# A graph network on one core: the attention of the second layer scaled by its sums on ScalarE, block by block, with other opening loads and a new order of steps

## The chip, the core and the metric

The kernel runs on one core of one Trainium2 chip. Its time is the device time of one execution in microseconds (us); the figure to be compared is the median of several executions. The core's engines each work through their own instruction queue, in order: TensorE (PE in the profile, PEld for its weight loads), VectorE (DVE), ScalarE (ACT), GpSimd (POOL) and SyncE (SP), which here issues nearly all DMAs.

## What is computed

`x` is 128 graphs of 128 nodes with 256 features in fp32; `adj` holds zeros and ones. Two layers follow each other. Cut to what matters:

```python
# layer 0, a graph transformer: 8 heads of 32
q, k = x @ Wq + bq, x @ Wk + bk
attn = softmax(q k^T / sqrt(32))
out  = sum over r of (attn * (adj == r)) @ (x @ Wv[r] + bv[r])
x = ln(x + out @ Wo + bo)
x = ln(x + gelu(x @ W1 + b1) @ W2 + b2)          # 256 -> 1024 -> 256
# layer 1: two graph attentions, then a feed-forward part
def gat(h, W, a):
    Wh = h @ W
    e = leaky_relu(Wh @ a[:256] + (Wh @ a[256:])^T, 0.2)
    att = softmax(where(adj > 0, e, -9e15), axis=1)
    return att @ Wh
h = ln(x + gat(gat(x, W1, a1), W2, a2))
out = ln(h + relu(h @ w_ff1 + b_ff1) @ w_ff2 + b_ff2)
```

## The kernel before

**Tiles.** The 16,384 nodes are worked through in 32 groups of 512 (four graphs, called blocks, of 128 rows). All weights stay on the core. The projections and both feed-forward parts (FFN) are done in a Strassen-Winograd form: seven products of half matrices in place of eight, with sums and differences on DVE and ACT around them. Each product is two matmuls of 128x256 (four records in the trace, 0.86 us) or, in the second half of an FFN (`po`, `seeded` at L534), eight of 128x128 (16 records, 1.78 us).

**PSUM.** Eight banks: two buffers of tag "s", used in turn by scores, `pw`, `py`, `pg`, `pwo`; single ones "qa" and "qb" (projections, and half of the scores), "fa" and "fe" (the FFN's `ph`, `po`), "av" (`pav`) and `seeded`.

**Steps of a group g.** `in` and `rest` load xT (L226), adj and x through SyncE. `q` projects q, k (`pqqa`, `pqqb`) and v (`pvqa`, `pvqb`; ACT copies at L806). `a` is layer 0's attention, for two blocks at a time (p = 0, 1): score matmuls `ps` (L859) into four banks, four exps on ACT (L866), masks on DVE (L876), weighted sums `pav` (L975), output projection `pwo` (L1021). `d` makes the softmax's denominators: 24 small DMAs on SyncE (L899: es, ea, pm from e), own rows by ACT copies (L903), sums on DVE. `n0` to `n3` are layer norms (L416 adds a result to x, L407 statistics, L431 a power on POOL, L465 planes for a transposing DMA), `t0` to `t2` the transposed copies (L493). `f` and `fc` are the first FFN (gelu) and its chain, `k` and `kc` the second (relu): L584 copies a bank to `p7`, L629 to `p16`, L621 and L648 seed a bank, L650 copies 256 columns to seed the output products, L549 is bias and activation. `gelu` and `exp` load ACT's function table.

**Layer 1's attention** is step `l` (`layer1`, `edges`). `pw` (L1098) gives Wh and the two score columns, ACT copies them to `wh` (L1103); the target column is spread over all partitions (for most groups through a tile in HBM: own, a DMA out, a DMA back that lands in `spread`; for the last groups by matmuls, `pr`). Then `edges` makes the weights of all four blocks in one tile `gs`: L1069 four ACT passes add source and target, L1073 leaky relu on DVE, L1075 exp on ACT, L1079 four DVE passes mask and sum, L1085 and L1086 bound and invert the sums, and L1087 multiplies the whole 128x512 tile by the reciprocals in one DVE pass. Then `py` (L1111, one matmul a block) applies the first attention, L1115 copies to `yh`, `edges` runs again, and `pg` (L1124) applies the second, two blocks to a bank; L416 adds it to x.

**Order.** Each step is a generator that goes on by one piece each time it is named. Three strings name them in the order in which their instructions go into the engines' queues: FRONT (L123) for the start, STEADY (L147) repeated for g = 1 to 29 with relative group numbers (`k:-1` is the second FFN of the group before, `q:2` the projections of the second group on), TAIL (L162) for the end. In a steady period the groups overlap: while group g is in its FFNs and layer 1, g+1 is in its attention, and g+2 in its projections.

In the trace the exps of group g+1 (p = 0), the output products of g's first FFN, and `pg` of the group before stand beside each other. TensorE's order there is `ps`, `po7` (16 matmul records), `pg` p = 0, `pvqa`, `pg` p = 1, `pvqb`, `seeded`; ACT's is the exp of `gs`, four exps of `e`, L806, L650, the four copies of L903.

**Opening.** The first weights and group 0's xT (512 KB, L226) go through SyncE's queue, the biases bq, bk, the two value biases (`bvs`, `b0`) and `bo` through ACT's. Eight matmul records (L1166) run ahead of the first projection `pq`, while these are on their way. Loads under names with `L` in the strings are lists worked off piece by piece.

Of the kernel before, what the change touches and what calls it, by code (L numbers as in the profile page):

```python
# [120 lines left out]


FRONT = """  # L123
Lqk in:0 Lqk q:0 Lqk Lv q:0 L1 q:0 Lv q:0 Lqk L1 in:1 Lv q:0 Lv_ q:0*2 Lv q:0 rest:0 Lv_ a:0*3 L1
q:0 d:0 a:0 Lv_ a:0 d:0 a:0*2 d:0 L1*2 d:0 q:0 d:0*2 Lh1 d:0 a:0 d:0 a:0 q:0*2 rest:1 q:0*2
rest:0 wqk a:0*7 q:1 L2 w1 a:0 L4 a:0*3 q:1*2 d:0 bo:0 d:0 Lgat Lg1 a:0*2 d:0*2 q:1 L2 Lg1 d:0 w1
d:0 q:1 bo:0 q:1 q:0 d:0 Lo q:1 d:0 q:0 q:1 bo:0 a:0*4 L1 a:1 a:0*2 a:1 a:0 rest:1 wqk w1 a:0
a:1*2 a:0 a:1 L3 a:1 Lg1 d:1 a:0 d:1 Lg1 d:1 a:1 a:0*2 q:1 a:0*2 Lg2 d:1 Lgat n0:0 b1 d:1*2 L2
a:1 d:1 n0:0 q:1 b1 q:1 n0:0 L4 q:1 wqk d:1 q:1 Lgat n0:0 a:1 b1 output_bias n0:0 wv L2 q:1
n0:0*2 t0:0 b1 a:1 output_bias t0:0 a:1 Lh1*2 a:1*3 Lgat a:1*2 gw f:0 a:1 t0:0 a:1 b1 L3 a:1 b1  # L130
w2 a:1 t0:0 w1 t0:0*2 d:1 fc:0 b1 gw q:1 Lg2 d:1*3 a:1 f:0 fc:0 f:0 b1 f:0 a:1 fc:0*3 d:1 L4 d:1
f:0 q:1 fc:0 f:0 fc:0 f:0 d:1 f:0 Lh2 gw L3 a:1 f:0 d:1 a:1 f:0*2 a:1 fc:0 a:1 fc:0*2 bo:1 w2
bo:1 fc:0*2 a:1*3 f:0 a:1 wqk fc:0 in:2 fc:0 gw a:1 L3 f:0 a:1 fc:0 f:0 fc:0*2 a:1 f:0 w2 a:1 Lh1
bo:1 a:1 L3 a:1 f:0 fc:0*3 f:0 wv n0:1 L3 fc:0 q:2 f:0 fc:0 c1 fc:0 f:0 n0:1 q:2 fc:0 w2 n0:1
fc:0 q:2 n0:1 t0:1 n0:1 f:0 c1 t0:1 fc:0 f:0 L4 fc:0 c1 n0:1 fc:0 wv fc:0 f:0*2 n0:1 q:2 fc:0 q:2
f:0 fc:0*2 q:2 n1:0*2 gw n1:0 Lh2 n1:0 q:2 t0:1 n1:0*2 c1 n1:0 q:2 t0:1 c1 u1 f:1 q:2*3 t0:1 c1
f:1 t1:0*2 c1 l:0 gelu u2 fc:1 t1:0 l:0 t0:1 t1:0 l:0*2 fc:1 f:1 l:0 fc:1 l:0*2 fc:1 l:0 q:2 l:0
f:1*3 fc:1*3 f:1*3 fc:1 rest:2 fc:1*2 q:2*2 exp q:2 fc:1 l:0*2 u1 l:0 q:2 u1 q:2 f:1 q:2 l:0 fc:1
f:1 l:0 a:2 l:0 u2 l:0 fc:1 l:0*3 a:2 f:1 fc:1*2 a:2 l:0 fc:1 l:0 a:2*2 l:0*3 a:2 l:0*2 u2 u1 d:2
l:0 d:2 l:0 fc:1 f:1 l:0 f:1 wv f:1*2 fc:1*2 l:0 d:2 fc:1 l:0 d:2 f:1 a:2 l:0 u2 q:2 l:0 fc:1 c1  # L140
l:0*2 fc:1 q:2 l:0*2 f:1 l:0*2 d:2*2 l:0 q:2 fc:1 q:2*2 l:0 f:1 d:2 q:2 l:0*2 q:2 l:0*2 q:2 l:0
n2:0 q:2*2 d:2 n2:0 fc:1*2 q:2 f:1 n2:0*2 d:2 fc:1 n2:0*2 a:2 fc:1 f:1 n2:0 fc:1 q:2 t2:0 f:1
rest:2 t2:0 q:2 fc:1 t2:0*2 fc:1 k:0 a:2 q:2 a:2*3 d:2 fc:1 f:1 kc:0 a:2 d:2 t2:0 a:2 k:0 f:1 a:2
k:0 a:2 k:0 a:2 t2:0 fc:1 a:2 d:2*2 kc:0 a:2 kc:0 a:2 d:2 a:2 k:0 a:2 k:0 d:2 n1:1 a:2 d:2 a:2
k:0 n1:1 k:0 kc:0
"""
STEADY = """  # L147
n1:0 k:-1 n1:0 kc:-1 n1:0 d:1*2 a:1 k:-1 kc:-1 d:1 a:1 kc:-1*2 bo:1 a:1 d:1 a:1 kc:-1 a:1*4
kc:-1*3 n1:0 in:2 kc:-1 n1:0 k:-1 t1:0*2 kc:-1 k:-1*2 t1:0 k:-1 l:0*2 k:-1 kc:-1*2 bo:1 t1:0
k:-1*2 l:0*2 kc:-1 a:1*2 kc:-1 l:0 kc:-1 l:0 a:1 kc:-1 l:0 kc:-1*2 l:0*2 kc:-1 k:-1 a:1 n0:1  # L150
kc:-1 k:-1 n0:1*2 kc:-1 k:-1 n0:1 bo:1 n0:1 q:2 k:-1 kc:-1 n0:1*2 kc:-1 l:0 kc:-1 l:0 k:-1
kc:-1*2 q:2 l:0 q:2 l:0*2 t0:1*2 q:2 kc:-1 l:0 rest:2 f:1 k:-1 l:0 t0:1*2 q:2*2 l:0*2 fc:1 q:2
gelu l:0 t0:1 l:0 f:1*3 t0:1 l:0*2 fc:1 l:0 f:1 l:0*3 k:-1 q:2 f:1 fc:1 l:0 kc:-1 l:0 f:1 fc:1
f:1*2 q:2 n3:-1 l:0 fc:1*3 q:2 fc:1 f:1 fc:1*3 q:2 fc:1*2 f:1 q:2 f:1 q:2 n3:-1 fc:1*2 f:1*2 q:2
l:0 fc:1 l:0*2 f:1 q:2 l:0 fc:1*2 f:1 n3:-1 fc:1 l:0 q:2 fc:1 q:2*2 f:1 fc:1 out:-1 l:0 a:2 fc:1
l:0*2 f:1 l:0*2 a:2*2 l:0 a:2*2 l:0 d:2 q:2 a:2 q:2 d:2*2 f:1 a:2 fc:1 l:0*4 d:2 l:0 n2:0 q:2
d:2*2 q:2 fc:1*2 q:2 n2:0 q:2 f:1 n2:0*3 q:2 d:2 fc:1 q:2 n2:0 q:2 d:2 f:1 n2:0 fc:1*2 q:2 d:2
f:1 fc:1 q:2 t2:0*2 a:2 t2:0*2 q:2 a:2 q:2 f:1 q:2 fc:1 t2:0*2 k:0 f:1 exp a:2 fc:1 kc:0 d:2
a:2*2 rest:2 a:2 k:0 kc:0 d:2 a:2 k:0*2 kc:0 a:2 k:0 d:2*2 a:2 d:2 a:2 d:2 a:2 fc:1 a:2*4 d:2 a:2
k:0 n1:1 kc:0 a:2 k:0 n1:1 k:0  # L160
"""
TAIL = """  # L162
n1:0 k:-1 kc:-1 n1:0*2 kc:-1 d:1*2 a:1 k:-1 kc:-1 a:1 d:1 k:-1 bo:1 a:1 kc:-1*4 d:1 kc:-1 n1:0
k:-1 n1:0 a:1 t1:0*2 k:-1 kc:-1 k:-1 l:0 bo:1 a:1 kc:-1 l:0*2 kc:-1 k:-1 l:0 kc:-1 a:1 t1:0 a:1
t1:0 l:0 a:1 k:-1 a:1 l:0 kc:-1*2 l:0*2 kc:-1 a:1 kc:-1 l:0 kc:-1 bo:1 k:-1 kc:-1*2 a:1*2 k:-1
kc:-1 n0:1*2 k:-1 n0:1*2 k:-1 n0:1 l:0 n0:1 l:0 n0:1 l:0 kc:-1 l:0 t0:1 k:-1 l:0 kc:-1 l:0 kc:-1
t0:1 kc:-1*2 l:0 k:-1 l:0 kc:-1 l:0 gelu l:0 f:1 t0:1 l:0 t0:1 k:-1 l:0 kc:-1 l:0 t0:1*2 l:0 f:1
fc:1*2 kc:-1 l:0 fc:1 f:1*2 k:-1 fc:1 f:1 n3:-1 l:0*2 fc:1 f:1*2 l:0 fc:1 n3:-1 l:0 fc:1 l:0 f:1
fc:1 f:1 l:0 fc:1 f:1 fc:1 l:0*2 fc:1 l:0 fc:1 l:0*3 fc:1*2 f:1*2 fc:1 f:1 l:0*4 fc:1 f:1 l:0
fc:1 f:1*2 fc:1 l:0*2 fc:1 l:0 fc:1 f:1 l:0*2 f:1 fc:1*2 n2:0 f:1 n2:0 fc:1*2 n2:0*2 fc:1 f:1  # L170
n2:0 f:1 n2:0*2 t2:0*2 fc:1*2 f:1 fc:1 t2:0 fc:1*2 f:1*2 fc:1*2 n1:1 t2:0 k:0 t2:0 k:0 kc:0 n1:1
t2:0 k:0 n1:1 k:0 n1:1 kc:0 n1:1 k:0 kc:0 n1:1*2 t1:1*2 kc:0 k:0*3 t1:1 k:0 l:1*2 t1:1 l:1 kc:0
n3:-1 l:1 kc:0*2 l:1*3 kc:0*2 l:1 kc:0 l:1 kc:0 k:0 kc:0 l:1*4 kc:0 l:1*3 k:0 l:1 kc:0 l:1 k:0*3
kc:0 l:1*5 kc:0 l:1 kc:0 k:0 l:1*5 k:0 l:1 kc:0 l:1 k:0 l:1*2 kc:0*3 l:1*2 kc:0 k:0 l:1*6 kc:0
k:0 l:1*3 kc:0 l:1*2 k:0 n2:1 kc:0 n2:1*5 kc:0*2 k:0 kc:0 n2:1 k:0 kc:0 k:0 t2:1*2 kc:0*2 k:1
t2:1*3 kc:1 t2:1 k:1 kc:1 k:1 checks k:1 kc:1 k:1 kc:1 k:1 kc:1 k:1 kc:1*2 k:1 kc:1*3 k:1 k:0
kc:1*2 kc:0 k:1*2 kc:1 k:1 kc:1*2 k:1 kc:1 k:1*2 kc:1 k:1*2 kc:1 n3:0 kc:1*2 k:1 kc:1 exp kc:1*2
n3:0*2 kc:1*2 out:-1 k:1*3 kc:1*3 k:1 kc:1 k:1 kc:1 out:0 k:1 z:1*2 kc:1*2 z:1*2
"""


# [8 lines left out]
def fast_pass(ctx, tc, a, out):  # L190
# [873 lines left out]
    def edges(target, source, S, l):  # L1064

        n = f"{S['g']}_{l}"
        S["att"] = s = w1p.tile([P, G, P], F32, tag="gs", name="gs_" + n)
        for b in range(G):
            nc.scalar.activation(  # L1069
                s[:, b, :], target[:, b, :], AF.Identity, bias=source[:, b, :]  # L1070
            )
# [15 lines left out]
        nc.vector.tensor_mul(s, s, rd[:, :, None].to_broadcast([P, G, P]))  # L1087
# [500 lines left out]
```

## Time and profile before

| | |
|---|---|
| three executions | 2609.13, 2611.95, 2613.82 us; median 2611.95 |
| the profiled execution | 2611.15 us, of which its span is 2609.4 |
| granted TensorE clock over the span | 0.997 |
| busy, of the span | PE 98%, PEld 88%, DVE 89%, ACT 72%, POOL 5% |
| DMA | 186 MB, of which 66 MB read from HBM; mean 71 GB/s |

The profile is of one execution. "Busy" of an engine is the time in which it has an instruction; a line such as `L1087 DVE ... 128x512 f32 x64 | 44.3, 692 | 2.2` gives the source line, the engine, the shapes, how many, then busy us, mean ns of one, and the engine's idle time just before them with what ended it. A wait line gives who waited for whom, us in total, times, and the longest. The chain follows the end of the work backwards, at each step to what released it. On PE the period from one group's `ps` to the next is 79.42 us on average over 28 periods (217.1 to 2440.8 us).

### The profile page before, as it was taken

To read this page: it belongs to the slowest core of one execution; us is meant where nothing else is said; L and a number is where in the kernel's file an instruction comes from. 1 tells how busy PE (TensorE), PEld (TensorE's weight loads), DVE (VectorE), ACT (ScalarE), POOL (GpSimd) and SP (SyncE) were. 2 spreads that over 40 slices of the span, in tenths; PEclk is the share of its full clock that TensorE was granted. 3 is DMA by queue.
4 is the path that set the end of the run, shared out by engine and by line. 5 is a ranking of instruction groups with operands and counts; after the bars stand their busy time and mean duration, and the time that the engine had idled before them with its cause. 6 is when DMAs were issued, how large, how long until landed. Compare 5 with 4: busy or idle time off the path is not lost.

```text
span 2609.4 us, 54584 instructions
## 1 busy us (share of the span) xinstructions
PE 2566.4 (98%) x20362; PEld 2286.5 (88%) x20362; DVE 2329.3 (89%) x6041; ACT 1883.0 (72%) x3841; POOL 142.1 (5%) x137
## 2 busy tenths in 40 slices
...
DMA packets 317375, 186.36 MB, mean 71 GB/s; under 512 B 230448, under 2 KB 272560, under 8 KB 317104
## 3 DMA queue, kind: packets, MB, share of 16 engines
...
q8 instruction: 162, 2.65, 0.4%
...
q10 hardware_dynamic: 1104, 0.40, 0.1%
...
## 4 chain that ended last, share of the span: by engine, by line
PE 83%; ACT 7%; DVE 5%; DMA 3%; issue 1%; SPq 1%; POOL 0%; DVEq 0%; ACTq 0%; POOLq 0%
PE ph L525 14%; PE po L534 14%; PE seeded L534 12%; PE seeded L525 11%; PE pqqa L789 4%; PE pvqa L789 4%; PE pav L975 4%; PE pw L1098 4%; PE pqqb L789 3%; PE pvqb L789 3%; PE pwo L1021 3%; ACT e L866 3%; PE ps L859 3%; PE pg L1124 2%; PE py L1111 2%; ACT hT L549 1%
## 5 line engine op out<-in xcount | busy, mean ns | idle before, releaser
L493 ACT COPY yT<-pT 128x512 uint16<-128x512 uint16 x384 | 271.3, 764 | 107.8 <-DMA pT<-planes 106.4
L465 ACT COPY planes<-x 128x512 uint16<-128x512 uint16 x384 | 218.3, 615 | 137.2 <-DVE x L445 135.5
L431 POOL TENSOR_TENSOR rs<-rs,mhalf 128x4 f32<-128x4 f32 x129 | 140.0, 1085 | 2406.7 <-DVE rs L430 1893.4
L525 PE MATMUL seeded<-yS,w_L_gnn_w_ff 128*128 128x256 f32 x768 | 203.5, 387 | 1.4 <-ACT p L629 0.7
L525 PE MATMUL seeded<-yS,w_L_gnn_W 128*128 128x256 f32 x768 | 199.9, 383 | 1.5 <-DVE hT L633 1.1
L525 PE MATMUL ph<-yT,w_L_gnn_W 128*128 128x256 f32 x768 | 198.1, 381 | 0.6 <-ACT yT L493 0.6
L407 DVE BATCH_NORM_STATS2 st<-x 128x6 f32<-128x256 f32 x512 | 190.1, 413 | 2.5
L534 PEld LDWEIGHTS po<-w_L_gnn_W,hT 128*128 128x128 f32 x1536 | 186.1, 192 | 6.7 <-ACT hT L549 2.1
L525 PE MATMUL ph<-yT,w_L_gnn_w_ff 128*128 128x256 f32 x768 | 187.7, 379 | 3.2 <-ACT seeded L648 2.1
L534 PE MATMUL po<-w_L_gnn_W,hT 128*128 128x128 f32 x1536 | 187.1, 275 | 1.7 <-ACT hT L549 1.7
L534 PE MATMUL po<-w_L_gnn_w_ff,hT 128*128 128x128 f32 x1536 | 187.1, 275 | 0.0
L534 PEld LDWEIGHTS po<-w_L_gnn_w_ff,hT 128*128 128x128 f32 x1536 | 181.7, 192 | 1.7
L525 PEld LDWEIGHTS seeded<-yS,w_L_gnn_w_ff 128*128 128x128 f32 x768 | 139.3, 190 | 38.2 <-ACT seeded L648 9.5
L876 DVE TENSOR_TENSOR pm<-e,adj 128x512 f32<-128x512 f32 x256 | 169.2, 682 | 0.4 <-ACT e L866 0.2
L525 PEld LDWEIGHTS seeded<-yS,w_L_gnn_W 128*128 128x128 f32 x768 | 142.8, 190 | 28.0 <-ACT seeded L648 6.4
L866 ACT ACTIVATE e<-ps 128x512 f32<-128x512 f32 x256 | 139.4, 602 | 34.8 <-PE ps L859 29.1
L525 PEld LDWEIGHTS ph<-yT,w_L_gnn_w_ff 128*128 128x128 f32 x768 | 143.5, 190 | 22.1 <-ACT seeded L648 2.5
L525 PEld LDWEIGHTS ph<-yT,w_L_gnn_W 128*128 128x128 f32 x768 | 141.7, 190 | 21.6 <-ACT seeded L621 1.2
L903 ACT COPY es<-e 32x512 f32<-32x512 f32 x240 | 147.1, 613 | 4.5
L549 ACT ACTIVATE hT<-hT,c_L_gnn_b_ff 128x256 f32<-128x256 f32 x256 | 115.9, 501 | 39.4 <-DVE hT L592 36.7
L621 ACT COPY seeded<-ph 128x512 f32<-128x512 f32 x64 | 37.4, 584 | 135.9 <-DVE x L667 135.2
L1098 PE MATMUL pw<-wu,yT 128*128 128x260 f32 x512 | 133.2, 389 | 2.3 <-ACT wh L1103 1.3
...
## 6 DMA issues: line engine op xcount, KB each, us to landing
...
```

Source lines behind the costliest of these rows:

```text
L407: nc.vector.bn_stats(st[:, b % 2, :], S["x"][:, b, :])
L431: nc.gpsimd.tensor_tensor(rs[:, bs], rs[:, bs], k.mhalf[:, bs], op=ALU.pow)
L465: nc.scalar.copy(planes[:, :, b], words)
L493: nc.scalar.copy(o.rearrange("p (b t h) -> p h b t", b=2, h=2), pT[:, :, :, c, :])
L525: nc.tensor.matmul(bank[:, s * TH : (s + 1) * TH], wa[:, form, 0, f * P : (f + 1) * P], m, start=start and s == 0, stop=True, skip_group_c ...
L534: nc.tensor.matmul(bank[:, s * P : (s + 1) * P], m[:, f, s * P : (s + 1) * P], wb_[:, form, f, :], start=start and s + f == 0, stop=True, ...
L549: nc.scalar.activation(o[:, s], o[:, s] if src is None else src[:, s * TH : (s + 1) * TH], func, bias=ba[:, f : f + 1],)
L789: nc.tensor.matmul(bank[:, s * TH : (s + 1) * TH], *ops, start=start and s == 0, stop=True, skip_group_check=True,)
L866: nc.scalar.activation(e[:, s], pss[s], AF.Exp, scale=SCALE)
L876: nc.vector.tensor_mul(pm[:, s], S["e", p][:, s], S["ad"][:, pair(p), None, :].to_broadcast([P, 2, NCH, P]),)
L903: nc.scalar.copy(es[own, 0], flat_e[own, s])
L1098: nc.tensor.matmul(pw[:, :NU], yT[:, c, b * P : (b + 1) * P], wu[:, c, :], start=(c == 0), stop=(c == NCH - 1),)
```

## The change

1. In `edges` the one DVE pass that multiplies `gs` by the reciprocal sums becomes four ACT passes (Identity with a scale read from the column of the block), one for each block of 128x128, in place. They form a piece of their own. Each counts on ACT's semaphore, and each `py` or `pg` matmul waits for its own block's pass. In the whole program DVE has 64 instructions fewer and ACT 256 more.
2. `bvs`, `b0` and `bo` go from ACT's queue to a list "b" on SyncE's queue, named three times as `Lb` in FRONT. The xT load of group 0 is issued as two DMAs of 256 KB. SyncE's first issues were Wq, xT, Wq, Wk, Wv; they are Wq, Wv, Wq, xT, xT, Wk, adj.
3. FRONT, STEADY and TAIL are new throughout. PE's count of instructions is the same. Around the lines above, by the program's order of instructions in a steady period (after's line numbers from L1087 on are higher by two):

| place | before | after |
|---|---|---|
| PE after `ps` p = 0 | po7, pg 0, pvqa, pg 1, pvqb, seeded | po7, pvqa, pg 0, pg 1, seeded, pvqb |
| ACT there | exp of gs, 4 exps of e, L806, L650, 4 x L903 | exp table, exp of gs, 4 exps of e, **4 scales of gs**, L650, L806, 4 x L903 |
| PE around `py` | py 0, seeded, py 1, py 2, ph7, py 3 | ph7, ph1, seeded, py 0, py 1, pqqb, py 2, py 3 |
| ACT after `ps` p = 1 | L621, 2 exps, p7, p16, exp, L549, exp, 4 x L903 | L621, 4 exps, p7, p16, L549, 4 x L903 |
| PE before `pav` p = 0 | seeded, ph1, pav | seeded (one earlier), ph1, seeded, pav |

In TAIL `pav` moves ahead of products that follow L648, and a gelu table load stands between the last exp of `gs` and the last scales; in FRONT the first scores of group 1 precede the second `pav` of group 0, and `py` and `pg` of group 0 have other work before them.

```diff
@@ FRONT, STEADY, TAIL: all tokens anew; STEADY's first lines
 STEADY = """
-n1:0 k:-1 n1:0 kc:-1 n1:0 d:1*2 a:1 k:-1 kc:-1 d:1 a:1 kc:-1*2 bo:1 a:1 d:1 a:1 kc:-1 a:1*4
-kc:-1*3 n1:0 in:2 kc:-1 n1:0 k:-1 t1:0*2 kc:-1 k:-1*2 t1:0 k:-1 l:0*2 k:-1 kc:-1*2 bo:1 t1:0
+kc:-1 d:1 k:-1*2 a:1 k:-1 kc:-1 a:1 d:1*2 n1:0 a:1*2 k:-1 n1:0 k:-1 n1:0 k:-1 a:1 kc:-1 a:1
+n1:0*2 d:1*2 a:1 d:1 bo:1 d:1 k:-1 a:1 kc:-1*4 a:1*3 in:2 a:1 kc:-1*3 n1:0*2 kc:-1*2 k:-1*2
...
@@ entered
-        nc.sync.dma_start(
-            xt, xT[:, g * T : (g + 1) * T].rearrange("(c p) t -> p c t", p=P)
-        )
+        cols = xT[:, g * T : (g + 1) * T].rearrange("(c p) t -> p c t", p=P)
+        for c in range(NCH) if g == 0 else (slice(0, NCH),):
+            nc.sync.dma_start(xt[:, c], cols[:, c])
         yield 1
@@ the weights' loads
     bq, bk = k.col("L0_gnn_bq"), k.col("L0_gnn_bk")
+    k.queue = nc.sync
+    to("b")
     bvs, bv = k.row("L0_gnn_bv", 2 * D, cut(2 * D)), k.tile([P, D], "bv")
     b0 = cut(NCH)
-    k.load(nc.scalar, b0, a["L0_gnn_bv"][0].rearrange("(c p) -> p c", p=P))
+    k.load(nc.sync, b0, a["L0_gnn_bv"][0].rearrange("(c p) -> p c", p=P))
     bo = k.row("L0_gnn_bo")
-    k.queue = nc.sync
     to("qk")
@@ edges
         nc.vector.tensor_scalar(rd, den, LO, None, op0=ALU.max)
         nc.vector.reciprocal(rd, rd)
-        nc.vector.tensor_mul(s, s, rd[:, :, None].to_broadcast([P, G, P]))
+        yield
+        for b in range(G):
+            nc.scalar.activation(s[:, b, :], s[:, b, :], AF.Identity, scale=rd[:, b : b + 1])
         yield 1
```

More of the change, by code (lines that the diff above doesn't have):

```diff
@@ L123 @@
 FRONT = """
[L124 to L145, printed above, removed]
+Lqk Lv Lqk in:0 Lqk rest:0 Lv Lqk Lv q:0 L1 q:0*2 Lv_ Lv q:0 in:1 Lb q:0*4 a:0 Lv_ L2 a:0*4 Lv_
+q:0 d:0 a:0 d:0 a:0 d:0 rest:0 d:0 Lb q:0 L1 d:0*2 Lg1 a:0 d:0*2 L1 a:0 Lb q:0*3 Lh1 a:0 q:0
@@ new lines @@
+a:0*5 bo:0 a:0*2 L1 a:0 q:1 L1 a:0 d:0 L1 a:0 bo:0 q:1 L2 q:1 d:0 Lgat*2 wqk d:0 q:1 rest:1 q:0
+a:0 q:0 d:0 q:1 d:0*3 Lo q:1 Lg1 Lgat q:1*2 a:1 a:0 a:1*2 w1 a:0 a:1 w1 Lg2 d:0 a:1 a:0 Lg1 gw
+a:1 a:0 a:1 d:1*2 a:0 d:1 a:0*4 Lg1 a:0*3 L4 d:1 q:1*2 a:0 d:1*2 L2 d:1 a:0 L3 d:1 rest:1 a:0 a:1
+n0:0 q:1 Lh1 q:1 b1 a:1 n0:0 q:1*2 b1 n0:0 b1 a:1 n0:0*2 w1 L4 a:1*2 wqk n0:0*2 a:1 w1 a:1 b1
+a:1*2 b1 t0:0 d:1 Lh1 t0:0 Lgat a:1*2 t0:0 L2 b1 t0:0 L3 output_bias f:0 output_bias d:1 bo:1 a:1
+L3 t0:0 q:1 fc:0 d:1 t0:0 f:0 a:1 wv fc:0 d:1*2 fc:0 a:1 f:0 b1 f:0 L4 q:1 Lh1 a:1 fc:0 w2 f:0
@@ new lines @@
+fc:0*2 b1 f:0 fc:0 f:0 gw f:0 fc:0*4 L3 f:0*2 fc:0 d:1 fc:0 f:0 fc:0 f:0 wv a:1 fc:0 u1 d:1*2 f:0
+a:1 f:0 w2 a:1 L4 bo:1 fc:0*2 f:0 w2 a:1*3 fc:0 f:0 a:1*4 w2 a:1 wqk L3*2 fc:0 f:0 in:2 fc:0
+a:1*2 q:2 c1 fc:0*2 a:1 f:0*2 n0:1 fc:0 u2 n0:1 q:2 n0:1 fc:0 q:2 fc:0 q:2 f:0 gw q:2 f:0 Lh2
+n0:1 gw q:2 c1 n0:1 fc:0 wv fc:0 f:0 Lg2 n0:1 fc:0*2 q:2 n0:1 t0:1 f:0 t0:1 f:0 fc:0 rest:2 bo:1
+q:2 t0:1 fc:0 bo:0 fc:0 n1:0*2 gw f:1 t0:1 n1:0 t0:1 c1 n1:0*2 c1 u2 q:2 fc:1 c1 n1:0*2 f:1 q:2*2
+f:1*2 c1 t0:1 q:2 t1:0 q:2 fc:1 t1:0 q:2 wqk fc:1 l:0 fc:1 t1:0 l:0*2 t1:0 l:0 f:1 u2 l:0*3 f:1
@@ new lines @@
+l:0 fc:1 q:2 l:0 u2 fc:1*2 f:1*2 q:2 c1 q:2 fc:1 gelu q:2 a:2 Lh2 fc:1 a:2 fc:1 l:0 q:2 l:0 f:1
+l:0*2 exp wv a:2 l:0*2 fc:1 a:2 f:1 fc:1 l:0*5 fc:1 a:2 l:0 u1 l:0 a:2 l:0*3 f:1 l:0*3 a:2 l:0 u1
+l:0 fc:1 f:1*2 fc:1*2 f:1 q:2 d:2 q:2 fc:1*2 q:2 f:1 d:2 fc:1 u1 f:1*2 c1 l:0 fc:1 l:0*3 fc:1 q:2
+d:2 l:0 fc:1 l:0*4 f:1 l:0 fc:1 q:2 l:0 q:2 l:0 f:1 fc:1 q:2 d:2 fc:1 l:0 d:2 l:0*2 d:2 l:0*3 d:2
+n2:0 d:2 n2:0*2 q:2 n2:0 q:2 fc:1 q:2 n2:0*2 q:2 f:1 d:2 fc:1 f:1 n2:0 t2:0 f:1 fc:1 t2:0 fc:1
+q:2 a:2*2 q:2 f:1 fc:1 a:2 t2:0 a:2*2 rest:2 fc:1 t2:0 k:0 f:1 a:2 kc:0 d:2*2 t2:0 a:2*2 t2:0 d:2
@@ L146 @@
+a:2 k:0 a:2*2 kc:0 k:0 fc:1 d:2 a:2*2
 """
 STEADY = """
-n1:0 k:-1 n1:0 kc:-1 n1:0 d:1*2 a:1 k:-1 kc:-1 d:1 a:1 kc:-1*2 bo:1 a:1 d:1 a:1 kc:-1 a:1*4
-kc:-1*3 n1:0 in:2 kc:-1 n1:0 k:-1 t1:0*2 kc:-1 k:-1*2 t1:0 k:-1 l:0*2 k:-1 kc:-1*2 bo:1 t1:0
-k:-1*2 l:0*2 kc:-1 a:1*2 kc:-1 l:0 kc:-1 l:0 a:1 kc:-1 l:0 kc:-1*2 l:0*2 kc:-1 k:-1 a:1 n0:1
-kc:-1 k:-1 n0:1*2 kc:-1 k:-1 n0:1 bo:1 n0:1 q:2 k:-1 kc:-1 n0:1*2 kc:-1 l:0 kc:-1 l:0 k:-1
-kc:-1*2 q:2 l:0 q:2 l:0*2 t0:1*2 q:2 kc:-1 l:0 rest:2 f:1 k:-1 l:0 t0:1*2 q:2*2 l:0*2 fc:1 q:2
@@ L153 @@
[L153 to L158, printed above, removed]
@@ L159 @@
-a:2*2 rest:2 a:2 k:0 kc:0 d:2 a:2 k:0*2 kc:0 a:2 k:0 d:2*2 a:2 d:2 a:2 d:2 a:2 fc:1 a:2*4 d:2 a:2
-k:0 n1:1 kc:0 a:2 k:0 n1:1 k:0
+kc:-1 d:1 k:-1*2 a:1 k:-1 kc:-1 a:1 d:1*2 n1:0 a:1*2 k:-1 n1:0 k:-1 n1:0 k:-1 a:1 kc:-1 a:1
+n1:0*2 d:1*2 a:1 d:1 bo:1 d:1 k:-1 a:1 kc:-1*4 a:1*3 in:2 a:1 kc:-1*3 n1:0*2 kc:-1*2 k:-1*2
+t1:0*2 kc:-1 k:-1*2 t1:0 k:-1 t1:0 l:0*2 k:-1*2 l:0 kc:-1 bo:1 l:0 a:1 kc:-1 a:1 kc:-1 bo:1 a:1
+kc:-1*2 a:1 l:0 n0:1 l:0*4 k:-1 kc:-1*2 n0:1 kc:-1 q:2 k:-1 n0:1 kc:-1*2 n0:1*3 k:-1*2 q:2
```

41 lines of the change are left out of this document (25 added, 16 removed).

## The prediction, made before the changed kernel ran

> **What bounds the kernel now.** I read the page's first part, then windows by stage, then the waits, then the chain around one wait.
>
> ```profile
> PE 2566.4 (98%) x20362; PEld 2286.5 (88%) x20362; DVE 2329.3 (89%) x6041; ACT 1883.0 (72%) x3841; POOL 142.1 (5%) x137
> ...
> PE 83%; ACT 7%; DVE 5%; DMA 3%; issue 1%; SPq 1%; POOL 0%; DVEq 0%; ACTq 0%; POOLq 0%
> ```
>
> TensorE is busy 98% of the span and is 83% of the chain that ended last. The change takes no matmul away, so at most the other 43 us can be won. Where they lie shows in the windows (stretch, length, then busy time of PE, weight loads, DVE, ACT and POOL, granted clock, DMA share, GB/s):
>
> ```profile
> 0.00:30.00 30.00, 25.44 (x190) 15.14 (x191) 11.69 (x32) 12.07 (x21) 0.70 (x6) 1.00 0.72 202
> 120.00:150.00 30.00, 25.17 (x145) 21.02 (x144) 22.36 (x64) 17.24 (x34) 1.01 (x1) 0.94 0.16 39
> 200.00:2440.00 2240.00, 2231.01 (x17813) 2001.61 (x17812) 2042.55 (x5271) 1661.59 (x3393) 122.38 (x113) 1.00 0.32 71
> 2500.00:2590.00 90.00, 82.23 (x494) 70.85 (x493) 64.67 (x184) 56.24 (x121) 5.08 (x5) 0.98 0.14 24
> ```
>
> In the steady part, 28 periods of 79.42 us, PE shows 9 us idle in 2240; DVE is at 91%, ACT at 74%. The opening (4.6 us idle), the first layer 1 (4.8) and the tail (7.8) hold more per microsecond. One wait of the weight loads comes back in every group:
>
> ```profile
> PEld pg L1124 <- ACT e L866: 10.8, 29, 0.4
> ...
> PE pg L1124 <- ACT e L866: 6.1, 29, 0.2
> ```
>
> The chain around one of the 29 (start, length, what):
>
> ```profile
> 1007.92 1.14 PE ps L859 x32
> 1009.06 2.06 ACT e L866 x4
> 1011.12 0.10 issue
> 1011.22 1.10 PE pg L1124 x4
> 1012.32 0.86 PE pvqa L789 x4
> 1013.18 0.86 PE pg L1124 x4
> ```
>
> The score matmuls fill both "s" banks of PSUM, four exps empty them, and pg, which wants such a bank, follows. The 16 po matmuls between (1.79 us, left out of the chain) end 0.37 us before pg starts; pg's first matmuls are 0.07 slow besides. By the row, 10.8/29 = 0.37; with 0.07, **0.44 us per group, 12.8 us in all**, is what an order can win here.
>
> **The change, part by part.** The prices:
>
> ```profile
> L1087 DVE TENSOR_TENSOR gs<-gs,gr 128x512 f32<-128x512 f32 x64 | 44.3, 692 | 2.2
> ...
> L549 ACT ACTIVATE hT<-hT,c_L_gnn_b_ff 128x256 f32<-128x256 f32 x256 | 115.9, 501 | 39.4 <-DVE hT L592 36.7
> ...
> L1069 ACT ACTIVATE gs<-spread,wh 128x128 f32<-128x128 f32 x124 | 56.1, 522 | 14.7 <-DMA spread<-hbm 14.1
> ...
> L1069 ACT ACTIVATE gs<-pr,yh 128x128 f32<-128x128 f32 x8 | 2.3, 373 | 0.2 <-PE pr L1051 0.2
> ```
>
> *Scaling.* 64 DVE passes of 692 ns go, 44.3 us; 256 ACT passes over 128x128, in place, with a pointer operand, come. No row shows this one. Below, L1069 out of PSUM: 373 ns, four in 1.14 us. Above, L1069 with its strided input: 522 ns, four in 1.77. Nearest is L549, in place, with a pointer, on 256 columns: 501 ns, four in 1.71, so one each 0.40. Copies of 512 and 256 columns (L584 582 ns, L650 377) give 0.80 ns a column, so 128 columns less are 0.10 less: 0.40 us for the first, 0.30 for each further, **1.30 for four** (ends 1.14 and 1.77). Two sets a group: 2.6 us more ACT work in 79.4, where ACT idles 20.5 (26% of the steady stretch); 1.4 less DVE. What counts is who waits.
>
> The page "ScalarE: Activation LUTs" of the Trainium skill speaks against the move: its rules for kernel authors give multiplications to VectorE. Its prices ("What ACT_TABLE_LOAD costs": 186 ns, 93 per pointer, 0.833 a column, 93 overlapped) make an estimate of 0.39 + 3 x 0.29 = 1.27 us against 0.69 for the one DVE pass; the 373 ns of L1069 agrees. By engine time alone the change would thus lose 0.6 us a set, 37 us in all; these sit on an engine with idle time, so I count waits instead.
>
> *pg.* In the new steady order pvqa (0.86 us) goes between po and pg; its bank is another one. PE then asks for pg at 1011.70 on the clock of the chain above, 0.58 after the exps ended, so the 0.44 goes. But the four scales for pg stand behind those exps in ACT's queue: done at 1011.5, 1011.8, 1012.1 and 1012.4, against matmuls that want them at 1011.7, 1012.15, 1012.6 and 1013.0. Hidden, by 0.2 to 0.6; at 522 ns and 0.41 apart (1011.64 to 1012.87) still by 0.06. Without this cover a group would lose up to 0.9 (0.40 + 0.5 of queueing). Queued behind the scales are the copy of L650, done near 1012.7 where a product wants it at 1013.43, then the copies L806 and es. Per-block semaphores help: pg starts after one block. *py* (the other set): first scale ready some 0.55 us before PE asks for py; DVE's reciprocal that it waits for, 0.6 to 0.8 before.
>
> *New order in the second FFN.* Before, two exps, then the copy p7 (L584), p16 (L629), an exp, two hT passes, the last exp. Now four exps stand ahead of p7. Exps start each 0.49, so p7 moves from 1033.11 to 1034.1 and ends at 1034.7, where PE wants it at about 1034.65: I take 0.05 late plus 0.1 for refilling, **0.15 a group** (ends 0 and 0.5). Two p16 copies and one L648 copy keep 0.03 to 0.15 of cover: 0.05 together. es follows the last exp at once and starts about 0.2 earlier, so the denominators' DMAs (es, ea, pm on SyncE) aren't later. The moved steps take their loads and stores along (in, rest, out on SyncE, still issued a group ahead; 4.1 us to land), and POOL's one steady step, rs L431, is 5% of its time: 0. DVE's chain from pg to the last L416 before pw is some 40 us of work nearly without a hole; pg reaches it 0.2 later and no hole of mine opens: 0.
>
> Steady sum: -0.44 + 0.15 + 0.05 = -0.24; times 29, **-7.0** (ends: all won, -12.8; 0.1 lost a group, +3).
>
> *Opening loads.* bvs, b0 and bo leave ACT's queue for SyncE's list, and xT of group 0 is two DMAs behind three weight loads, where it was second. The first pq starts at 6.64, when the eight warm-up matmuls end. SyncE issued at 0.74, 1.20, 1.66 and then 3.35; the 256 KB of bvs took 4.7 us from issue to landing. Issued at 3.35, the first half of xT lands at 8.05, 1.4 late; issued at 2.1, in time: 0 to +1.4. In the first layer 1 py comes sooner after pw (8.4 us of filler for a chain of about 11.6, where it was 11.5), pg later (11.7 for about 13, where 8.2). So PE waits 3.2 + 1.3 = 4.5, in place of 5 idle and 1.5 at half speed: in 120:150 the eight pg records take 526 ns on average (393 else), at clock 0.94 after a 2.3 us hole. That is -2. Against it, group 1's first scores now precede group 0's second pav: +1 to +2 on kT and pwo, and up to +1.4 for xT. I take **0, from -5 to +5**.
>
> The half-speed row is what "TensorE: Matmul & The Clock Gate" (Part 1) describes, but with an idle window of about 3.4 us; here 2.3 were enough. Were the page's figure the point, the new 3.2 wait would be cheap; by the row it may cost 1.5.
>
> *Tail.* A wait of 2.28 at 2472.9 for L648 gets pav (1.88 us) as filler: -0.9 to -1.9. Where the scaling itself is on the chain (before the last pg, 0.70 then a 0.02 issue), the first block's 0.40 saves 0.3. One gelu table load (1.28) now stands between the last exp and the last scales, beside 1.3 of DVE masks: +0.15. **-1.5, from -3.5 to +0.5.**
>
> Sum: -7.0 + 0 - 1.5 = -8.5, against the profiled execution's 2611.15 (span 2609.4 and 1.75 around it; 0.8 below the median of three): **2602.6 us**.
>
> **Rivals.**
> - *All of it won.* p7 is in time: -12.8 - 1.5 and a point in the front, 2596. For it: p7's margin is less than I can read from starts. Against: four tight copies at once.
> - *Given back.* DVE is at 91%; if the chain from pg to pw is the real bound, the 0.44 returns as a longer wait of pw for L416 (now 0.2 in some iterations), and the front or tail pays a little: 2610. Against: few pw waits in the trace of before.
> - *Slower: ACT's queue in the second FFN.* If the four exps start later than 0.07 after ps ends, p7, p16 and L648 all come late, each 0.15 plus 0.1 refill: 0.75 against the 0.44 won, +0.31 x 29 = 9 us: 2620. It decides from about 0.1 us later than I read, or if scales at 0.41 apart push the same copies. For it: no slack there over 0.15. Against: 20 us idle on ACT a group.
>
> **Chances.** The forecast's case 0.43 (2594 to 2607), all won 0.14, given back 0.25, slower 0.18. Measurement tells 0.2% (5 us) from no change: faster 0.57, same 0.25, slower 0.18. The range: below, all won with the tail's and front's best, 2611.15 - 12.8 - 3.5 - 5 = 2590; above, the slower case, 2620.
>
> **What would show it.** Right: no pg wait on e in the new waits, scales near 400 ns and 0.30 apart, a period near 79.2. Wrong: pg or py waiting for the scales; a new row of ph waiting for p L584 far over 5 us in all; pw waiting for L416 in every group; more than 5 us idle before 30 us. I am wrong in kind if the period doesn't fall though the pg wait has gone.

## The result, and the profile after

The changed kernel takes 2626.57 us (median of 4, 2624.32 to 2628.15); the kernel before, run beside it, 2612.18. The ratio is 1.0054, with a 95% interval of 1.0041 to 1.0067: **slower by 14 us**, where 2602.6 and a range up to 2620 were forecast.

The first part of its page and the chain's shares by engine:

```profile
PE 2575.7 (98%) x20362; PEld 2288.0 (87%) x20362; DVE 2291.0 (87%) x5977; ACT 1943.7 (74%) x4099; POOL 145.0 (6%) x137
...
PE 79%; DMA 6%; DVE 6%; ACT 6%; SPq 2%; issue 1%; POOL 0%; ACTq 0%; DVEq 0%; POOLq 0%
```

ACT carries 61 us more and DVE 38 less; neither is where the time went. The chain is: PE's share fell from 83% to 79%, and DMA's rose from 3% to 6%. Something on PE's way now hangs on transfers. Where, by stage (columns as in the windows of before):

```profile
0.00:30.00 30.00, 25.40 (x189) 14.99 (x190) 11.26 (x31) 11.80 (x21) 0.70 (x6) 1.00 0.66 189
...
120.00:150.00 30.00, 27.31 (x180) 23.73 (x175) 20.45 (x59) 23.18 (x50) 1.38 (x1) 1.00 0.18 40
150.00:200.00 50.00, 47.54 (x408) 41.83 (x407) 47.15 (x127) 35.60 (x73) 2.48 (x3) 0.97 0.36 80
200.00:2440.00 2240.00, 2227.23 (x17713) 1992.09 (x17713) 1997.32 (x5183) 1697.94 (x3589) 124.68 (x113) 1.00 0.31 70
```

The same 2240 us hold 100 matmuls fewer than before (17713 against 17813). Taken between the starts of the first `ps` of successive groups, a period is 79.88 us where it was 79.42. Over the 28 periods that is +13.0 us; the start up to the first of these `ps` lost 2.65 (216.39 against 213.74; the 217.1 given for the kernel before is the `pg` behind it), the end from the last of them won 2.44. Start and end are of one execution each: in the other runs below with the changed kernel's FRONT and loads the same point lies anywhere from 214.2 to 218.3 us. The steady part is the result.

The waits of the whole run that matter, two of DVE among them (who for whom: us in total, times, longest):

```profile
DVE x L416 <- PE pg L1126: 21.5, 32, 0.7
...
PEld pvqa L789 <- DVE v L831: 15.0, 24, 1.4
...
PEld pw L1100 <- ACT wh L1105: 10.3, 25, 1.0
PEld ph L525 <- ACT p L584: 10.0, 32, 0.8
PEld seeded L525 <- ACT p L629: 9.6, 35, 0.5
...
DVE pm L908 <- DMA pm<-e: 5.0, 12, 1.3
```

`pg` for the exps is gone, as forecast. Two waits that before had little or no part are there instead. The rows of the weight loads don't say what the matmuls lose: for pvqa the weight loads waited 15.0 us, while 11.8 (0.42 a group) is missing between the starts of matmuls. What they lose shows in the spacing of these starts against the undisturbed 0.216 us. Worked out so from the starts in both traces, us a group:

| what PE's next matmul waited for | before | changed |
|---|---|---|
| pg for the exps (with refilling) | 0.45 | 0 |
| pvqa (last product) for L831 | 0 | 0.42 |
| pw behind po, for the copy of wh | 0.06 | 0.35 |
| pw otherwise, refilling included | 0.19 | 0.11 |
| second FFN: ph, for p7 | 0 | 0.14 |
| second FFN: seeded, for p16, L633 or L648 | 0.28 | 0.47 |

That is 0.98 against 1.49, 0.51 more; the period grew by 0.46.

**The wait of pvqa.** DVE in one of the later groups, with the lines between left out (start, length, what, idle before it):

```profile
2148.34 0.69 DVE L908 TENSOR_TENSOR pm<-pm 128x512 f32<-128x512 f32 x1 [1.32 <-DMA pm<-e]
2148.94 0.88 DVE L445 SCALAR_TENSOR_TENSOR x<-x,mv,r_L_gnn_g_ln 128x256 f32<-128x256 f32 x2
...
2151.46 0.68 DVE L910 TENSOR_TENSOR es<-es,pm 128x512 f32<-128x512 f32 x1
2152.17 0.69 DVE L876 TENSOR_TENSOR pm<-e,adj 128x512 f32<-128x512 f32 x1
2152.78 0.68 DVE L831 TENSOR_TENSOR v<-pvqa,pv 128x512 f32<-128x512 f32 x1
```

and PE, which wants the bank that L831 reads:

```profile
2151.49 1.03 PE L789 MATMUL pvqb<-w_v,xT 128*128 128x256 f32 x4
2153.52 1.13 PE L789 MATMUL pvqa<-w_v,xS 128*128 128x256 f32 x4 [1.01 <-DVE v L831]
```

L908 adds what the DMAs from e brought. It waits 1.32 us for the last of them, and L831, nine places behind it in DVE's queue, is later by as much, though the bank that it reads has long been full. Over the 28 groups L908 starts 11.6 to 13.0 us after `ps` and L831 follows 4.45 later each time; PE can take up to about 16.2. In the kernel before, three instructions stand between the two (left out here):

```profile
1021.51 0.68 DVE L908 TENSOR_TENSOR pm<-pm 128x512 f32<-128x512 f32 x1
...
1023.37 0.68 DVE L831 TENSOR_TENSOR v<-pvqa,pv 128x512 f32<-128x512 f32 x1
1023.97 0.68 DVE L910 TENSOR_TENSOR es<-es,pm 128x512 f32<-128x512 f32 x1
```

There L908 starts at 13.66 in every group, to 0.01, and never waits, and L831 follows 1.86 later. The last of the DMAs that it needs lands 10.8 to 12.4 us after `ps` in that kernel and 11.0 to 12.7 in the changed one: the landing moved by 0.65 on average, the add by 2.0. L831 would start at 16.07 even where L908 doesn't wait, so about 0.1 us is left for a late DMA.

**The wait of pw.** ACT in the changed kernel, and then in the kernel before:

```profile
1055.32 1.40 ACT L493 COPY yT<-pT 128x512 uint16<-128x512 uint16 x2 [0.94 <-DMA pT<-planes]
1056.58 0.36 ACT L1105 COPY wh<-pw 128x260 f32<-128x260 f32 x1
```

```profile
1047.83 0.77 ACT L493 COPY yT<-pT 128x512 uint16<-128x512 uint16 x1 [1.01 <-DMA pT<-planes]
1048.47 0.36 ACT L1103 COPY wh<-pw 128x260 f32<-128x260 f32 x1
1048.73 0.77 ACT L493 COPY yT<-pT 128x512 uint16<-128x512 uint16 x1
```

Before, the copy of wh stood between the two halves of yT; now it stands behind both, 0.63 us further from the DMA that they wait for. The second `pw` needs the bank that this copy empties, and starts at 1057.00, 0.39 after PE has become free:

```profile
1057.00 1.14 PE L1100 MATMUL pw<-wu,yT 128*128 128x260 f32 x4 [0.39 <-ACT wh L1105]
```

### The profile page after: what moved, and what is told of

It reads as the page before. It is cut to its first block, busy times and chain, and to the rows that moved or that the text cites. A ratio compares the mean times of both kernels' runs of the same rounds, so it can differ in the third digit from the quotient of the medians.

```text
span 2622.6 us, 54851 instructions
## 1 busy us (share of the span) xinstructions
PE 2575.7 (98%) x20362; PEld 2288.0 (87%) x20362; DVE 2291.0 (87%) x5977; ACT 1943.7 (74%) x4099; POOL 145.0 (6%) x137
## 3 DMA queue, kind: packets, MB, share of 16 engines
q8 instruction: 162, 2.65, 0.5%
## 4 chain that ended last, share of the span: by engine, by line
PE 79%; DMA 6%; DVE 6%; ACT 6%; SPq 2%; issue 1%; POOL 0%; ACTq 0%; DVEq 0%; POOLq 0%
PE ph L525 15%; PE po L534 12%; PE seeded L525 12%; PE seeded L534 10%; PE pav L975 4%; DMA pT<-planes 4%; PE pwo L1021 4%; PE pqqa L789 4%; PE pw L1100 4%; PE pqqb L789 3%; PE ps L859 3%; PE pvqa L789 2%; PE py L1113 2%; SPq L899 1%; DVE x L445 1%
## 5 line engine op out<-in xcount | busy, mean ns | idle before, releaser
L525 PE MATMUL ph<-yT,w_L_gnn_w_ff 128*128 128x256 f32 x768 | 196.6, 383 | 0.4 <-ACT p L584 0.4
L592 DVE TENSOR_TENSOR hT<-ph,p 128x512 f32<-128x512 f32 x128 | 87.7, 685 | 87.1 <-PE ph L525 86.4
L903 ACT COPY es<-e 32x512 f32<-32x512 f32 x240 | 147.0, 613 | 4.3
L549 ACT ACTIVATE hT<-hT,c_L_gnn_b_ff 128x256 f32<-128x256 f32 x256 | 115.8, 500 | 42.6 <-DVE hT L592 38.9
L866 ACT ACTIVATE e<-ps 128x512 f32<-128x512 f32 x256 | 132.6, 602 | 15.5 <-PE ps L859 6.3
```

The lines of the kernel that those rows point to most:

```text
L525: nc.tensor.matmul(bank[:, s * TH : (s + 1) * TH], wa[:, form, 0, f * P : (f + 1) * P], m, start=start and s == 0, stop=True, skip_group_c ...
L549: nc.scalar.activation(o[:, s], o[:, s] if src is None else src[:, s * TH : (s + 1) * TH], func, bias=ba[:, f : f + 1],)
L866: nc.scalar.activation(e[:, s], pss[s], AF.Exp, scale=SCALE)
L903: nc.scalar.copy(es[own, 0], flat_e[own, s])
```

## The experiments

All ratios are to the kernel before, run beside each on its chip, with 95% intervals. Theory A: the scaling is hidden by the new order, and the loss comes from where other steps were put, the two waits above. Rival B: the scaling on ACT is the loss.

### The scaling alone, and the order alone

`scale_only`: the kernel before with only the scaling changed.

```diff
-        nc.vector.tensor_mul(s, s, rd[:, :, None].to_broadcast([P, G, P]))
+        yield
+        for b in range(G):
+            nc.scalar.activation(s[:, b, :], s[:, b, :], AF.Identity, scale=rd[:, b : b + 1])
@@ orders: one more l token ahead of py and of pg
```

> The old orders and loads, only the scaling moved to ScalarE (in the steady order behind the four exps of e). Theory A, the new order made the loss and the scaling is cheap only where the order hides it: here pg follows the exps at once, so its first block comes about 0.4 us later a group; +9 to +13 us, 2621 to 2625. Rival B, the scaling itself is the loss of the changed kernel: +14 us or more, 2626. Rival C, it is hidden: 2612.

Measured: 2669.27 us, ratio 1.0218 (1.0204 to 1.0232), +56 us: at least four times what A expected, and by the number B's "14 or more". Its waits in PE's weight loads and matmuls:

```profile
PEld py L1113 <- ACT gs L1089: 44.4, 30, 1.6
...
PE py L1113 <- ACT gs L1089: 32.5, 29, 1.2
...
PEld pg L1126 <- ACT gs L1089: 22.1, 32, 2.4
...
PE pg L1126 <- ACT gs L1089: 15.2, 31, 1.7
```

pg's wait is 0.7 us a group (0.45 before), later for the scales as A said. The rest is py, by 1.3 us a group, which neither had counted. ACT's queue shows why:

```profile
1170.87 0.60 ACT L621 COPY seeded<-ph 128x512 f32<-128x512 f32 x1
1171.48 1.28 ACT L683 ACT_TABLE_LOAD   x1
1172.78 0.20 ACT L683 ACTIVATE none<-eps 1x1 f32<-1x1 f32 x1
1172.89 0.56 ACT L584 COPY p<-ph 128x512 f32<-128x512 f32 x1
1173.36 1.27 ACT L1089 ACTIVATE gs<-gs,gr 128x128 f32<-128x128 f32 x4
```

In the old order the gelu table load and the copy p7 stand between the mask and the scales. As long as the scaling was DVE's, they were beside py; on ACT they are ahead of it.

`order_dve`: the changed kernel with the scaling back on DVE.

```diff
+        nc.vector.tensor_mul(s, s, rd[:, :, None].to_broadcast([P, G, P]))
         yield
-        for b in range(G):
-            nc.scalar.activation(s[:, b, :], s[:, b, :], AF.Identity, scale=rd[:, b : b + 1])
```

> The changed kernel with its new orders and loads, but the scaling back in one DVE pass. Theory A: the loss stays, 2624 to 2632, with the same waits of pvqa for v (L831) and of pw for wh. Rival B: it falls back to about 2612.

Measured: 2626.46 us, ratio 1.0055 (1.0042 to 1.0069), the changed kernel's own; period 79.88 in both. Rival B falls, for the changed kernel: in the new order it makes no difference which engine scales. The page of the changed kernel has the price of it:

```profile
L1089 ACT ACTIVATE gs<-gs,gr 128x128 f32<-128x128 f32 x256 | 82.1, 404 | 1.8 <-DVE gr L1086 1.2
```

404 ns each, and four in 1.29 us in the timeline.

`gelu_later`: `scale_only` with the table load behind the scales in the steady order.

```diff
-... q:2 gelu l:0 t0:1 l:0 f:1*3 t0:1 l:0*3
+... q:2 l:0 t0:1 l:0 f:1*3 t0:1 l:0 gelu l:0*2
```

> The old orders with all scaling on ScalarE (as the run with the scaling alone, ratio 1.0218), and one step moved in the steady part: the gelu table load stands behind the first attention's scales, not ahead of p7 and them. Theory: py's wait of 1.28 us a group was that load of 1.28, and goes; the copies of yh behind the load are then late and give a part back, 0.4 to 0.9 a group: ratio 1.008 to 1.017. Rival: the scales wait for DVE's reciprocal and not for the load: ratio 1.020 or more.

Measured: 2665.78 us, ratio 1.0207 (1.0193 to 1.0221). By the ratio this is the rival's case, but the trace shows the theory's mechanism, with a size that was wrong: by the starts, py's wait for the scales fell from 1.28 to 0.24 us a group, but 0.9 came back at once as py's wait for yh, of which there was none, since the copies of yh now stand behind the load. In the changed kernel's trace the load stands behind those copies, too; that this is part of what makes the scaling free there is likely, and was not tried alone.

### The two waits

`wh_first`: the changed kernel with the copy of wh between the halves of yT.

```diff
-t1:0 k:-1 t1:0 l:0*2
+t1:0 k:-1 l:0*2 t1:0
```

> The changed kernel; only ScalarE's copy of the first block of wh stands between the two last copies of yT, not behind both. Theory A: the wait of pw for that copy, 9.7 us in 28 groups, goes: -10 us, 2616.5. Rival, the next thing pw or pwo waits for is as late: 2624 to 2627.

Measured: 2619.82 us, ratio 1.0025 (1.0012 to 1.0037). pw's wait fell from 0.35 to 0.01 us a group, the period by 0.32.

`sums_later`: the changed kernel with L906 and L908 behind the second norm's passes.

```diff
-n2:0*2 f:1 d:2 f:1 fc:1 d:2 n2:0 q:2 n2:0 q:2 fc:1 d:2
+n2:0*2 f:1*2 fc:1 n2:0 q:2 n2:0 d:2*2 q:2 fc:1 d:2
```

> The changed kernel; only the two DVE adds of the denominators (L906, L908) stand behind the second norm's passes, some 2 us later. Theory A, they stood ahead of their DMAs' landing and held up L831, for which pvqa waits: the wait of 9.5 us and 2.2 of refilling in 28 groups goes, -12 us, 2614.5. Rival, DVE is the bound and the wait only moves on to pav or the next one: 2624 to 2627.

Measured: 2622.84 us, ratio 1.0035 (1.0023 to 1.0047). L908 now starts at 13.61 in every group, and L831 at 16.47 where it was 16.07 to 17.48: the scatter goes, but L831 still comes 0.2 late, always. pvqa lost 0.25 us a group instead of 0.42. By the ratios that is 5 us (2 by the period of the profiled execution), less than half of what was expected, and the interval overlaps the changed kernel's.

`v_first`: the changed kernel with L831 ahead of L910 and the mask.

```diff
-q:2 fc:1 d:2 q:2 n2:0 a:2 q:2 f:1
+q:2 fc:1 q:2*2 d:2 n2:0 a:2 f:1
```

> The changed kernel; only DVE's L831 stands two passes earlier, ahead of L910 and the third mask, some 1.2 us. Theory A (the new steady order has two waits of its own, of pvqa for L831 and of pw for wh): nearly all of the 11.7 us of pvqa's wait and refilling in 28 groups goes; as the removal of the other wait brought 6.8 of 10, I expect -8, 2618. Rival, DVE is the bound and the time comes back at pav or at pw for L416: 2625.

Measured: 2617.2 us, ratio 1.0038 (1.0025 to 1.0052). On this chip the kernel before took 2607.71, so by the ratio the gain is 4 us, with intervals that overlap; by the period, which fell by 0.33, it is 9. No wait of pvqa for L831 is left. A small new wait appears (ph for yS, L502).

`wh_v`: both together.

> The changed kernel with both repairs, wh's first copy between the copies of yT and L831 two passes earlier. Theory A: the two add up, -6.8 - 8 = -15, 2611 to 2612, a period of about 79.35. Rival, one is given back at the other's place: 2617 to 2620.

Measured: 2610.82 us, ratio 1.0006 (0.9997 to 1.0015), a period of 79.43, the one of before (79.42). Theory A holds in sum, by the ratio to the kernel before on its chip (2607.71): two places in the order, four tokens, are 12 of the 14 us.

### What makes the adds late

`pg_first`: `order_dve` with pg ahead of pvqa again.

```diff
-l:0 out:-1 q:2 l:0 a:2 d:2 a:2 l:0 d:2 a:2 f:1 d:2 a:2 l:0*2 fc:1 q:2
+l:0 out:-1 l:0 a:2 d:2 a:2 l:0 d:2 a:2 f:1 d:2 a:2 l:0 q:2 l:0 fc:1 q:2
```

> The changed kernel's orders and loads with the scaling in one DVE pass, and pg ahead of pvqa again, as before. Theory: the wait of pg for the exps, 0.44 us a group, is back in full and nothing else goes, since pvqa's later wait for L831 hangs on DMAs and not on pg: +9 to +13 us against the new order with DVE scaling, ratio 1.009 to 1.0105. Rival: putting pvqa ahead of pg delays DVE and so made the new waits; then they shrink and the ratio is 1.0055 or less.

Measured: 2634.39 us, ratio 1.0087 (1.0073 to 1.0101), +8 against `order_dve`, just below the theory's range. pg's wait came back with 0.46 us a group, for DVE's multiplication now. pvqa's fell from 0.32 to 0.08, as the rival said, but not for its reason: L831 comes no sooner (16.74 us after `ps` on average, 16.50 in `order_dve`). PE, held up at pg, asks for the bank 0.53 later (17.58 where it is 17.05 undisturbed). Nor does pvqa ahead of pg make DVE much later: L416 reads pg 4.92 us after `ps` in `order_dve` and in the changed kernel, 4.76 in `pg_first`, 4.67 in the kernel before. The 0.71 us that DVE waits for pg in the changed kernel (the row of L416 above) are the place of the multiplication that it no longer does; `order_dve` waits 0.08 there.

`out_late`: the changed kernel with the store of `out` behind the denominators' twelve DMAs on SyncE; the next load of x, which takes over that buffer, a little later too.

```diff
-l:0 a:2 l:0 out:-1 q:2
+l:0 a:2 l:0 q:2
-fc:1 q:2 l:0*2 d:2 l:0 fc:1 d:2*2 l:0 fc:1 rest:2 n2:0
+fc:1 q:2 l:0*2 d:2 out:-1 l:0 fc:1 d:2*2 l:0 fc:1 n2:0
-q:2*3 n2:0 f:1 t2:0 k:0
+q:2*3 n2:0 rest:2 f:1 t2:0 k:0
```

> The changed kernel with one store moved on SyncE: out of 512 KB, which the new order issues 1.3 us after ps starts and straight ahead of the twelve DMAs of es and pm, stands behind them (and the next x load a little later). Theory, the store makes these DMAs land late and so holds up L908 and L831: most of pvqa's irregular wait goes, -4 to -8 us, ratio 1.0025 to 1.004. Rival, the train of twelve issues takes its 8 to 9 us with or without the store (it does so in the kernel before, where the store stands 2 us ahead of ps) and only DVE's order is at fault: ratio 1.0045 to 1.0065.

Measured: 2611.07 us, ratio 1.0011 (1.0001 to 1.0020; the kernel before took 2607.41 on this chip): by the ratios 11 us from one store and one load, the largest single step. SyncE in the kernel before, in the changed kernel, and with the store moved:

```profile
1005.88 0.39 SPq L1135 DMA_DIRECT2D out_dram<-x  x1
1009.66 0.54 SPq L899 DMA_DIRECT2D es<-e  x1
1010.25 1.23 SPq L899 DMA_DIRECT2D pm<-e  x2
```

```profile
1016.51 0.39 SPq L1137 DMA_DIRECT2D out_dram<-x  x1
1017.02 0.54 SPq L899 DMA_DIRECT2D es<-e  x1
1017.60 1.45 SPq L899 DMA_DIRECT2D pm<-e  x2
```

```profile
1018.47 1.23 SPq L899 DMA_DIRECT2D pm<-e  x2
1019.80 0.53 SPq L1137 DMA_DIRECT2D out_dram<-x  x1
```

L908's latest start falls from 13.03 to 12.66, its mean from 12.16 to 11.87; pvqa's wait falls from 0.42 to 0.18 us a group, and pw's by a third. In the kernel before, the store was issued 2 us ahead of `ps` and 3.8 ahead of the first of the twelve. The run moves store and load together. The traces point to the store: right behind it the first two of the twelve land 2.9 and 2.6 us after their issue on average, where it is 1.95 and 2.0 in the kernel before and with the store moved; the load is issued behind the last of the twelve. Which of the two counts for pw, whose yT comes by later DMAs, stays open.

`wh_v_out`: this and both repairs.

> The same with both repairs (wh's first copy earlier, L831 two passes earlier; ratio 1.0006 without the moved store). Theory: with L831 out of the way of L910 little is left to win, -0 to -2 us, ratio 0.9998 to 1.0008. Rival: the later x load or the denser DMAs cost it, ratio above 1.0015.

Measured: 2605.23 us, ratio 0.9991 (0.9982 to 1.0000). There was more left than expected; the new order thus repaired is level with, or a shade below, the kernel before. The gains overlap: 12 us from the two orders with the transfers left as they are, 11 from the transfers with the orders left, 16 from both, where the loss was 14. A late DMA costs only where something that PE needs stands close behind its wait.

### The rest

`all_three`: `wh_v` with the copy p7 after two of the four exps.

```diff
-a:2 kc:0 a:2*3 d:2*2 k:0 a:2 k:0 a:2
+a:2 kc:0 a:2*2 d:2*2 k:0*2 a:2*3
```

> The changed kernel with both repairs and the copy p7 after two of the four exps, as in the old order. Theory A: p7's place costs the 4.0 us of late ph matmuls in 28 groups, so 3 to 4 less than with two repairs: 2608. Rival, the scheduling of p7 is neutral and L629 or es is later for it: 2612.

Measured: 2611.36 us, ratio 1.0020 (1.0011 to 1.0029), no faster than `wh_v` and perhaps slower. The lateness of ph for p7 is gone (0.18 us a group to nothing), but the pav burst of the second half now takes 2.14 us where it took 2.02: given back at the next place.

`old_loads`: the changed kernel with the opening loads as before.

```diff
-    k.queue = nc.sync
-    to("b")
...
+    k.load(nc.scalar, b0, a["L0_gnn_bv"][0].rearrange("(c p) -> p c", p=P))
@@ FRONT: no Lb; Lqk in:0 Lqk Lv Lqk rest:0 ...
```

> The changed kernel with the opening loads as they were: bvs, b0 and bo on ScalarE's queue, xT of group 0 second and in one DMA. Theory: the opening loads are worth what the first score matmul shows, 13.66 us against 13.44, so this gives 0 to -1 us against the changed kernel, 2626 by the chip of the first runs (ratio about 1.005). Rival: the 2.7 us that the front lost come from the loads: ratio 1.004 or less.

Measured: 2625.14 us, ratio 1.0057 (1.0043 to 1.0071). The opening loads are not the loss. The first `ps` starts at 14.32 us with the old loads, at 13.66 in the changed kernel and at 13.44 before; but in the other runs with the changed kernel's opening it starts anywhere from 13.39 to 14.62, so no gain of theirs is shown either.

`before_pvqa`: the kernel before with pvqa ahead of pg, and nothing else.

```diff
-a:2*2 l:0 d:2 q:2 a:2 q:2 d:2*2 f:1
+a:2*2 d:2 q:2 l:0 a:2 q:2 d:2*2 f:1
```

> The kernel before with one product moved: pvqa between po and pg, as in the new order; scaling on DVE, old loads. What the prediction counted: pg's wait of 0.44 a group goes, -12.8 us, 2600. Theory A: DVE has to wait for pg some 0.2 to 0.7 us then and its queue runs later, so that part comes back at pw for L416: 2604 to 2610. Rival, all comes back: 2613.

Measured: 2598.15 us, ratio 0.9965 (0.9952 to 0.9979): **faster than both kernels**, by 9.6 us of the 12.8 that the prediction counted (the kernel before took 2607.71 on this chip). The first part of its page, and its chain's shares by engine:

```profile
PE 2561.3 (99%) x20362; PEld 2287.5 (88%) x20362; DVE 2328.2 (90%) x6041; ACT 1885.5 (73%) x3841; POOL 142.1 (5%) x137
...
PE 93%; DVE 3%; ACT 2%; DMA 1%; issue 1%; SPq 0%; POOL 0%; DVEq 0%; ACTq 0%; POOLq 0%
```

PE is 93% of the chain, and the period 79.09. Part of what came back is in the second FFN's seeded, which lost 0.35 us a group where it was 0.28, most of it now for L633, as DVE runs 0.25 us later from pg on.

`pvqa_scale1`: the same, with the second attention's scaling alone on ACT.

```diff
+        if l:
+            yield
+            for b in range(G):
+                nc.scalar.activation(s[:, b, :], s[:, b, :], AF.Identity, scale=rd[:, b : b + 1])
```

> The old orders with pvqa ahead of pg, and the scaling of the second attention alone in four ScalarE passes behind the four exps of e; the first attention's stays on DVE. Theory: pvqa hides these scales, 0.15 to 0.5 us ahead of each pg matmul, so the time stays that of the kernel with pvqa ahead alone, ratio 0.9965 within 0.001; DVE's 0.69 us a group less buys nothing. Rival: L650 and es behind the scales come late, +0.1 to 0.3 us a group: ratio 0.998 to 1.000.

Measured: 2607.56 us, ratio 0.9982 (0.9973 to 0.9991). No pg matmul waits for the scales, so they are hidden there as forecast; but by the ratios the time is some 4 us above `before_pvqa`, with intervals that just overlap, within the rival's range, though not at the rival's places. Its profile's period is longer by 0.19, of which 0.13 is in six groups where ph waits for ACT's copies of yT; the start, too, is 4.5 us longer in that one execution. Why just those groups was not tried.

## Why the prediction was wrong

- **pg's wait: right.** The 0.44 us a group was there to be won: 0.45 is gone in the changed kernel, and `before_pvqa` turned that one move into 9.6 us.
- **The scaling: right, in this order.** 0.40 us and 1.30 for four were worked out; 404 ns and 1.29 were measured. It costs nothing there (`order_dve`) and 56 us in the old order, where py and pg stand behind ACT's queue (`scale_only`, with the scales where that run put them). The Trainium skill's page "ScalarE: Activation LUTs" ("Rules for kernel authors") gives multiplications to VectorE; engine time agrees (1.29 us on ACT against 0.69), the kernel's time does not follow it. What decides is what is ahead of the scales in the queue.
- **"The moved steps take their loads and stores along (...): 0." This step failed.** It priced the transfers by their being a group ahead, not by what they newly stand in front of. The store of out went from 2 us ahead of `ps` to right before the twelve DMAs that a DVE add waits for; with the load that follows it that was 11 us (`out_late`).
- **"No hole of mine opens: 0." This step failed with it.** pg does reach DVE late by what was said (0.25 us, put at 0.2). But the chain was followed from pg to pw alone, not at the denominators' add L908, which the new order moves from 13.66 to 11.63 us after `ps`, into the time in which its DMAs land, with eight instructions between it and L831 where three stood. pvqa waits behind L831, 0.42 us a group; with L831 two places earlier that is gone (`v_first`). The rival "given back" named DVE's queue, and the wrong cause and place: pw for L416, a DVE at its bound, where it was pvqa for L831 behind a DMA.
- **A wait that was not looked for:** the copy of wh behind both halves of yT, 0.35 us a group (`wh_first` takes it away). The sum has no term for it, though the order of these three instructions stood in the two programs.
- **p7 and p16: in part.** p7 was put at 0.15 and came to 0.14; p16 and the L648 copy were put at 0.05, and seeded, which waits for them and for L633, lost 0.19 more. The slower rival rested on these; they are a third of the new waits, and taking p7's away (`all_three`) won nothing.
- **Front and tail: inside their ranges, in the front by luck.** +2.65 and -2.44. But py did not wait 3.2 us in the first group, and xT was not late; other waits (2.5 for L663, 1.2 for L648) stood in their place, and behind the first of these TensorE ran at half speed again (granted clock 0.50 from 155.2 to 158.6 us).

Added up by the table, 0.53 us a group was won and 1.04 lost, 0.51 in sum; the period shows 0.46. With both orders and the transfers put right (`wh_v_out`) the period is 79.18, where the sum had 79.2: the terms that were set to nothing, and the one left out, are what was missing.
